# Half-token scans for the first and last image, LayerNorms in lanes of their own, one activation ring, residuals by rows and ranking by image in a scheduled Mamba block

## The chip, the cores and the metric

The kernel runs on one core of one Trainium2 chip. The metric is device time in microseconds (us) of one execution. Times quoted are medians of an experiment's runs with their range. All runs here were in the same state (none of the slow kind), so runs are compared as they are. Sets of runs fell on different chips; the kernel before, run in each set, had medians of 3881 to 3885 us. Engines: PE is TensorE (PEld its weight loads), DVE is VectorE, ACT is ScalarE, POOL is GpSimd.

## The reference, cut to what matters

Eight images of 384 channels and 32x32 pixels (1024 tokens) pass through a Mamba block with an MLP; then five of them pass through an FFN with binarised weights and absmax quantisation.

```python
x = x + conv_block(_ln_c(x))                  # images of 384 x 1024, 8 of them
# inside conv_block (a second LayerNorm comes first):
xz = t @ in_proj_w.T                          # 384 -> 2 x 768
xm, z = jnp.split(xz, 2, axis=-1)
xc = silu(causal_conv3(xm) + conv_b)
dbc = xc @ x_proj_w.T                         # dt (24), B (16), C (16)
dt = softplus(dt @ dt_proj_w.T + dt_proj_b)
dA = exp(dt * A); dBu = dt * xc * B           # 768 channels x 16 states
def step(hst, inp):                           # over 1024 tokens
    hst = dA_t * hst + dBu_t
    return hst, einsum('bdn,bn->bd', hst, C_t)
y = (ys + xc * D) * silu(z)
t = y @ out_proj_w.T
t = gelu(t @ mlp_w1.T + mlp_b1) @ mlp_w2.T + mlp_b2   # 384 -> 1536 -> 384
# the FFN, on images 0 to 4, each a group with its own absmax
h = quantise(_ln_t(t) @ sign(W1 - mean).T + b1)       # 384 -> 1536
t = t + quantise(gelu(h) @ sign(W2 - mean).T + b2)    # 1536 -> 384
def quantise(a):                              # gamma is the max of |a| over one image
    return clip(a * 128 / (gamma + 1e-5), -128 + 1e-5, 128 - 1e-5)
```

## The kernel before

The kernel writes its operations down as a list (`Plan.add`), each with an engine, a cost in us and the tiles that it reads and writes. `Plan.run` then simulates the engines with these costs and emits the instructions of each engine in the order that the simulation finds. The order is then fixed in the program.

```python
MM = 0.86            # us for one product of 128 x 512
SIGNAL = 0.1
LOAD_TABLE = 1.29
...
def choose(e, now, able):                      # in Plan.run
    able = [op for s, op in able if s <= now]
    ...
    if e in ("DVE", "POOL"):
        able = [op for op in able if op.prio[0] > 0] or able
    return min(able, key=lambda op: op.prio)
...
def write_down(self):
    for b in range(B):
        plan.prio = (1,);  self.s1(b)          # LayerNorm, in_proj, convolution, dt, z
        plan.prio = (0,);  self.s2(b)          # the scans
        plan.prio = (2,)
        if b == 0: self.binarise("W1", KC, HID); self.binarise("W2", KH, C)
        self.s3(b)                             # out_proj and MLP
        if b < NQ: self.ffn(b)
```

Tiles come from rings of buffers; MLP, FFN and binarisation share three of them:

```python
"back": ring("back", 3), "t_b": ring("t_b", 3), "w_b": ring("w_b", 3),
"w6": ring("w6", 3), "res": ring("res", 3), "small": ring("small", 24),
```

A scan tile is 32 channels x 4 states on the partitions, 1024 tokens long. ScalarE makes the exponentials into PSUM, GpSimd the products dtx x B, VectorE scans and multiplies by C, and TensorE sums the states, two tiles to a group of sums. There are 96 tiles an image, 768 in all, in 384 groups of sums. Names in the profiles: da are the exponentials and then the scanned states, u the products before and after a scan, py the sums, yg the gated result of the scans; p_in and p_z are the two parts of in_proj, p_out is out_proj, p_h and p_o are the two products of the MLP, p_y and p_y2 those of the FFN; w_b and w6 are weights; p_sum and p_r belong to a LayerNorm.

```python
self.act(... AF.Exp, 1.12, r=[dt_r], w=[da], table="exp", scale=...)      # da is in PSUM
add("POOL", 2.36, lambda: nc.gpsimd.tensor_mul(u.real, dtx_r.real, bq.real))
add("DVE", 2.29, lambda: nc.vector.tensor_tensor_scan(
    da.real, da.real, u.real, 0.0, ALU.mult, ALU.add))
add("DVE", 1.21, lambda: nc.vector.tensor_mul(u.real, da.real, cq.real))
...
self.plan.prio = (-1,)
add("PE", 0.9, sums, r=hcs, w=[py])            # four matmuls, the fold over states
```

The ends of the FFN, shortened: a maximum over all partitions by GpSimd, and the residual of half an image in one instruction. With `lock`, the simulation keeps VectorE and GpSimd apart.

```python
def quant_scale(self, mx, n):
    nc.vector.tensor_reduce(m1.real, mx.real, AX.X, ALU.max)
    nc.gpsimd.partition_all_reduce(m2.real, m1.real, P, bass_isa.ReduceOp.absmax)
    ...
# at the end of ffn, for each half image
self.clip(yh, parts, q2)                       # GpSimd
add("DVE", c_dve(KC * T), lambda: nc.vector.scalar_tensor_tensor(
    x1.real, yh.real, q2.real[:, 0:1], x1.real, ALU.mult, ALU.add
), r=[q2, *parts], w=[x1], lock=True)          # 128 x 1536
```

## Time and profile before

| kernel before | |
|---|---|
| time, median of 4 runs | 3880.9 us (3879.5 to 3887.7) |
| first scan begins | 158.6 us |
| scan stage (first scan to last product behind a scan) | 3542.4 us, VectorE busy 3065.3, idle 477.1 |
| tail (after the last product) | 182.2 us, TensorE busy 161.6, VectorE 5.3 |
| granted TensorE clock, mean | 0.914 |

The page and the views that show this stand in the prediction below. The way of reading is the sum: time = first scan + VectorE's work in the scan stage + VectorE's idling in it + tail. It holds exactly, because the stages follow each other, and it says for every microsecond in which of four terms it was won or lost. Two groups of the kernel before that the prediction does not show matter later; they are by form, with busy us and mean ns after the first bar:

```profile
L885 DVE SCALAR_TENSOR_TENSOR x<-y,q,x 128x1536 f32<-128x1536 f32 x10 | 29.4, 2943 | 35.8 <-POOL y L809 35.6 <-DMA x<-mid_d 0.2
...
L774 DVE TENSOR_TENSOR w<-w,sgn 128x1535 f32<-128x1535 f32 x3 | 5.3, 1757 | 0.1
```

The first is the FFN's residual, ten instructions of 2.9 us; the second a part of the binarisation. Both read two operands from SBUF.

### The profile page before, as it was taken

The numbers are of one execution on the slowest core, as the hardware profiler recorded it, in microseconds if no ns is written. First come the engines' busy times: TensorE is split into PE (matmuls) and PEld (weight loads), VectorE is DVE, ScalarE is ACT, GpSimd is POOL, SyncE is SP. The second block draws the span as 40 slices with busy tenths as digits, with TensorE's granted clock in tenths as the row PEclk, the third lists the DMA queues.
The fourth block names the chain that finished last, engine by engine and source line by source line (L and its number), as shares of the span: only waits on it lengthen the run. The fifth ranks groups of instructions, "written<-read, shape, count | busy, mean of one in ns | idle before, by whom it ended". The sixth has DMA issues, their size and how long they took to land. (4 is left out here: it accounts for less than half of the span.)

```text
span 3883.2 us, 31296 instructions
## 1 busy us (share of the span) xinstructions
PE 3359.5 (87%) x9928; PEld 1275.0 (33%) x9928; DVE 3139.6 (81%) x2291; ACT 1925.0 (50%) x1991; POOL 2114.2 (54%) x1006
## 2 busy tenths in 40 slices
PE   5778878999999798987889978988879877999979
PEld 2223323333333233332233322333323322333334
DVE  5488888888888787897889977898778988899910
ACT  3456565757566665444345443453435443444411
POOL 0346655655555565655656565564666566566600
PEclk7888889999999899998999978998889988999989
DMA  7856667666677676646575564646565456666432
GB/s 252 250 158 205 195 194 250 218 210 198 195 258 245 196 225 196 218 145 204 171 221 174 190 198 154 222 152 206 171 195 179 156 193 192 210 190 189 149 83 81
DMA packets 344740, 746.16 MB, mean 192 GB/s; under 512 B 31488, under 2 KB 100608, under 8 KB 344576
## 3 DMA queue, kind: packets, MB, share of 16 engines
q1 hardware_dynamic: 342704, 743.30, 60.5%
q8 instruction: 79, 1.29, 0.1%
q10 hardware_dynamic: 1872, 0.88, 0.1%
q14 instruction: 85, 0.70, 0.1%
HBM read 560.55 MB, written 183.50 MB: 192 GB/s over the span
## 5 line engine op out<-in xcount | busy, mean ns | idle before, releaser
L628 POOL TENSOR_TENSOR u<-dtx_r,bc 128x1024 f32<-128x1024 f32 x768 | 1803.2, 2367 | 1308.2 <-PE py L643 1161.6
L631 DVE TENSOR_TENSOR_SCAN da<-da,u 128x1024 f32<-128x1024 f32 x768 | 1757.5, 2288 | 261.3 <-ACT da L396 205.8
L396 ACT ACTIVATE da<-dt_r,a_neg 128x1024 f32<-128x1024 f32 x768 | 851.8, 1115 | 977.7 <-DVE u L634 957.3
L634 DVE TENSOR_TENSOR u<-da,bc 128x1024 f32<-128x1024 f32 x768 | 936.6, 1220 | 32.7 <-DVE da L631 1.4
L643 PE MATMUL py<-u,fold 128*32 128x512 f32 x3072 | 547.1, 648 | 242.8 <-DVE u L634 239.2
L380 PE MATMUL p_h<-t,w_b 128*128 128x512 f32 x1152 | 531.8, 613 | 37.1 <-DMA w_b<-in_mlp_w 36.9
L380 PE MATMUL p_o<-g,w 128*128 128x512 f32 x1152 | 511.9, 598 | 0.0
L380 PE MATMUL p_y<-gf,w 128*128 128x512 f32 x720 | 336.9, 623 | 13.3 <-ACT gf L396 13.3
L380 PEld LDWEIGHTS p_h<-t,w_b 128*128 128x128 f32 x1152 | 217.1, 194 | 347.0 <-issue 298.5
L380 PE MATMUL p_y<-tn,w_b 128*128 128x512 f32 x720 | 326.1, 605 | 0.0
L396 ACT ACT_TABLE_LOAD x237 | 304.1, 1283 | 33.5 <-DVE xc L518 17.7
L380 PEld LDWEIGHTS p_o<-g,w 128*128 128x128 f32 x1152 | 213.6, 190 | 295.0 <-issue 284.6
L380 PE MATMUL p_z<-t,w_f 128*128 128x512 f32 x576 | 275.1, 629 | 24.5 <-DMA w_f<-in_in_proj_w 15.2
L380 PE MATMUL p_in<-t,w_f 128*128 128x512 f32 x576 | 271.5, 627 | 26.8 <-ACT t L396 14.8
L380 PE MATMUL p_out<-yg,w 128*128 128x512 f32 x576 | 271.9, 627 | 12.9 <-DMA yg<-yg_d 12.9
L643 PEld LDWEIGHTS py<-u,fold 128*32 128x32 f32 x3072 | 77.8, 111 | 621.8 <-DVE u L634 377.0
L396 ACT ACTIVATE g<-p_h,v_mlp_b 128x512 f32<-128x512 f32 x192 | 128.2, 681 | 192.1 <-PE p_h L380 192.0
L380 PEld LDWEIGHTS p_y<-gf,w 128*128 128x128 f32 x720 | 139.7, 199 | 216.5 <-issue 187.1
L380 PEld LDWEIGHTS p_y<-tn,w_b 128*128 128x128 f32 x720 | 135.0, 193 | 185.7 <-issue 156.1
L396 ACT ACTIVATE y<-p_y,v_b 128x512 f32<-128x512 f32 x150 | 101.9, 683 | 176.9 <-PE p_y L380 136.2
L558 POOL TENSOR_TENSOR xc<-xc,dt 128x512 f32<-128x512 f32 x96 | 118.6, 1269 | 119.0 <-ACT dt L396 119.0
L704 DVE SCALAR_TENSOR_TENSOR res<-p_o,v_mlp_b,res 128x512 f32<-128x512 f32 x48 | 35.2, 733 | 175.5 <-PE p_o L380 175.4
(75 smaller groups left out, 2132.8 us busy)
## 6 DMA issues: line engine op xcount, KB each, us to landing
dt_r<-dt_d SPq DMA_DIRECT2D x192, 512.0 KB, 5.3
dtx_r<-dtx_d SPq DMA_DIRECT2D x192, 512.0 KB, 4.7
w_f<-in_in_proj_w SPq DMA_DIRECT2D x192, 192.0 KB, 3.2
w_b<-in_mlp_w SPq DMA_DIRECT2D x192, 192.0 KB, 3.4
w<-in_mlp_w SPq DMA_DIRECT2D x96, 384.0 KB, 4.0
bc<-rows_d SPq DMA_DIRECT2D x64, 512.0 KB, 6.0
y_d<-y SPq DMA_DIRECT2D x120, 256.0 KB, 3.6
gf<-y_d SPq DMA_DIRECT2D x20, 1536.0 KB, 9.0
```

The lines of the kernel that those rows point to most:

```text
L380: self.nc.tensor.matmul(p.real, w.real[:, k, :], t.real[:, k0 + k, :], start=start and k == 0, stop=stop and k == n - 1,)
L396: lambda: self.nc.scalar.activation(out(), in_(), func, **{k: v() if callable(v) else v for k, v in kw.items()}),
L558: add("POOL", c_pool(T), lambda k=k, xc=xc, dt=dt: nc.gpsimd.tensor_mul(xc.real[:, k, :], xc.real[:, k, :], dt.real[:, k, :]), r=[dt[k]], ...
L628: add("POOL", 2.36, lambda u=u, dtx_r=dtx_r, bq=bq: nc.gpsimd.tensor_mul(u.real, dtx_r.real, bq.real), r=[dtx_r, bq], w=[u])
L631: add("DVE", 2.29, lambda da=da, u=u: nc.vector.tensor_tensor_scan(da.real, da.real, u.real, 0.0, ALU.mult, ALU.add), r=[u], w=[da])
L634: add("DVE", 1.21, lambda da=da, u=u, cq=cq: nc.vector.tensor_mul(u.real, da.real, cq.real), r=[da, cq], w=[u])
L643: nc.tensor.matmul(py.real[p0 : p0 + DQ, :], self.fold, hc.real[:, cols], start=(q == 0), stop=(q == NQUAD - 1),)
L704: nc.vector.scalar_tensor_tensor(res.real, po.real, self.mlp_b2[:, m : m + 1], res.real, ALU.add, ALU.add)
```

## The change

Its intent: start the scans earlier and shorten the tail by scanning the first and the last image in two halves of 512 tokens, with the state carried over in a small tile; and let the order follow the images more evenly. LayerNorms get lanes (their own place in a ring's order), ranking holds the first stage of far-off images back, MLP and FFN share one large activation ring, and the FFN's residual is added by rows of 128 channels. The diff, cut to its core:

```diff
+SUMS = 1.2
...
+        def rank(op):
+            lane, b = op.prio[:2]
+            if lane <= 0:
+                first = (lane, b)
+            elif lane in (1, 4):
+                first = (1, b) if b <= scanned + 1 else (3, b)
+            else:
+                first = (2, b)
+            return (*first, op.prio[2])
...
-            "back": ring("back", 3), "t_b": ring("t_b", 3), "w_b": ring("w_b", 3),
-            "w6": ring("w6", 3), "res": ring("res", 3), "small": ring("small", 24),
+            "yg": ring("yg", 1), "hid": ring("hid", 1), "t_b": ring("t_b", 1), "w_b": ring("w_b", 4),
+            "w6": ring("w6", 2), "res": ring("res", 3),
+            "t_n": ring("t_n", 2), "w6_n": ring("w6_n", 2), "small": ring("small", 12),
...
     def s1(self, b):
+            with self.plan.lane(4):
+                self.load(t, lambda x: x, src, size=4 * P * KC * T)
+                self.norm(t, self.eps_m, (1.0 + E2) / C)
...        (z of the first half is now made between the two dt stages)
     def s2(self, b):
+        if b in (0, B - 1):
+            state = self.piece("state", [P, NJ * NQUAD], "state")
+            for half in range(2):
+                self.scan(b, half, state)
+        else:
+            self.scan(b, None, None)
...        (scan_tile: a tile of a half scan is two blocks of 512 columns)
+        for k, col in enumerate(cols):
+            add("DVE", 0.13 + n * 0.0021, lambda k=k, col=col: nc.vector.tensor_tensor_scan(
+                to.real[:, k, :], da.real[:, k, :], u.real[:, k, :],
+                state.real[:, col : col + 1] if half else 0.0, ALU.mult, ALU.add,
+            ), ...)
+        if half == 0:
+            add("ACT", 0.25, lambda: nc.scalar.copy(state..., to.real[:, :, n - 1]), ...)
...
-                add("PE", 0.9, sums, r=hcs, w=[py])
+                    add("PE", SUMS, sums, r=hcs, w=[py])
...        (binarise)
+            first = self.dram["dtx", 0][0]
+            self.load(w, lambda t: t, src[:, i * kk : (i + 1) * kk, :], r=[first], ...)
...        (ffn)
+            with self.plan.lane(6):
+                ... self.norm(t, self.eps_f, 1.0 / C)
...
-            add("DVE", c_dve(KC * T), lambda yh=yh, x1=x1: nc.vector.scalar_tensor_tensor(
-                x1.real, yh.real, q2.real[:, 0:1], x1.real, ALU.mult, ALU.add
-            ), r=[q2, *parts], w=[x1], lock=True)
+            for m in range(KC):
+                add("DVE", c_dve(T), lambda m=m, yh=yh, x1=x1: nc.vector.scalar_tensor_tensor(
+                    x1.real, yh.real[:, m, :], q2.real[:, 0:1], x1.real, ALU.mult, ALU.add
+                ), r=[q2, yh[m]], w=[x1], lock=True)
...        (write_down: priorities carry the image, FFN and binarisation are lane 5)
```

## The prediction

> **What bounds the kernel now.** I read the page from the top: busy shares, the slices, the chain, the groups. First the shares and the slices (busy tenths of forty 97 us slices):
>
> ```profile
> PE 3359.5 (87%) x9928; PEld 1275.0 (33%) x9928; DVE 3139.6 (81%) x2291; ACT 1925.0 (50%) x1991; POOL 2114.2 (54%) x1006
> ...
> PE   5778878999999798987889978988879877999979
> ...
> DVE  5488888888888787897889977898778988899910
> ...
> PEclk7888889999999899998999978998889988999989
> ```
>
> TensorE and VectorE are both nearly full and neither is full throughout. VectorE is empty in the last two slices and both are half empty in the first. So I asked for busy time by stretch: up to the first scan (158.6 us), from there to the last product behind a scan (3701 us), and the rest. Columns: stretch, length, then busy us (and instructions) of PE, PEld, DVE, ACT, POOL, then granted clock, DMA share, GB/s.
>
> ```profile
> 0.00:158.60 158.60, 99.71 (x238) 42.92 (x238) 68.99 (x123) 55.94 (x69) 17.80 (x20) 0.74 0.78 254
> 158.60:3701.00 3542.40, 3098.26 (x9330) 1161.95 (x9330) 3065.33 (x2161) 1837.03 (x1887) 2095.10 (x986) 0.92 0.61 195
> 3701.00:3883.20 182.20, 161.57 (x364) 70.13 (x364) 5.25 (x7) 32.01 (x35) 1.26 (x1) 0.93 0.32 87
> ```
>
> The reader sees three stages: a head of 159 us before any scan, a scan stage of 3542 us in which VectorE works 3065 us and idles 477 us, and a tail of 182 us that is TensorE alone. What the scan stage is made of stands in the groups (busy, mean ns of one, idle before and what ended it):
>
> ```profile
> L631 DVE TENSOR_TENSOR_SCAN da<-da,u 128x1024 f32<-128x1024 f32 x768 | 1757.5, 2288 | 261.3 <-ACT da L396 205.8
> L634 DVE TENSOR_TENSOR u<-da,bc 128x1024 f32<-128x1024 f32 x768 | 936.6, 1220 | 32.7 <-DVE da L631 1.4
> ```
>
> Scan and product take 1757.5 + 936.6 = 2694 of VectorE's 3140 us. Of its 477 us of idling in this stage the waits view names most:
>
> ```profile
> DVE da L631 <- ACT da L396: 205.8, 78, 13.9
> ...
> DVE m L798 <- POOL m L793: 65.5, 10, 9.6
> ...
> DVE x L885 <- POOL y L809: 35.6, 5, 7.6
> ...
> DVE xr L652 <- PE py L643: 33.1, 21, 5.9
> ```
>
> The tail is read from the chain that ended last, in order of time: the last yg goes out and comes back, then two image halves pass through TensorE, one after the other.
>
> ```profile
> 3707.17 8.56 DMA yg<-yg_d
> 3715.78 17.51 PE p_out L380 x36
> 3733.29 15.46 PE p_h L380 x36
> 3748.77 9.00 DMA w_b<-in_mlp_w
> 3757.91 13.46 PE p_h L380 x24
> 3771.37 30.90 PE p_o L380 x72
> 3802.27 15.45 PE p_out L380 x36
> 3817.72 30.90 PE p_h L380 x72
> 3848.62 30.91 PE p_o L380 x72
> ```
>
> My reading: in the scan stage VectorE is the bound, helped to its idling by TensorE, whose static order also serves MLP and FFN; in the tail TensorE is.
>
> **What the Trainium skill says.** (1) "TensorE: Matmul & The Clock Gate", Part 1 (the HAM clock gate): an idle array falls back to half its clock, activity releases it. The trace agrees: the stretch from 2700 to 2800 us with PE busy 74.7 of 100 us had a granted clock of 0.78, the one from 3400 to 3500 us with 98.4 had 1.00. So evening out TensorE's work saves some of its time. (2) "GPSIMD Engine Reference", section 2.1 Instruction dispatch: a freshly loaded library kernel costs about 6 us without a visible instruction. Here each PARTITION_ALL_REDUCE takes 0.41 us but GpSimd stands idle 5.85 us before the last one and 7.16 us after it; that is where the 65.5 us of "DVE m" come from. (3) "ScalarE: Activation LUTs", What ACT_TABLE_LOAD costs: about 1283 ns each, which is the page's mean (237 of them). The ACT lists before and after hold the same number of loads, 238, so nothing is gained there.
>
> **The change part by part.** The orders of instructions of both kernels are what I used besides the trace.
>
> Tail. With the last image scanned by halves, the order after the last sums holds one half (18 matmuls p_out, 36 p_h, 36 p_o) where there were two. In the trace the second half took 15.45 + 30.90 + 30.91 = 77.3 us. So the tail falls from 182 to about 105 us: 15 us of yg out and back, 17.5 + 15.5 + 13.5 + 30.9 = 77.4 us of matmuls, the rest for waits on weights, GELU and the last store. Gain: some 77 us, the surest part.
>
> Head. Image 0 starts on its first half. Before, dtx of the first half was ready at 76 us, dtx of the second went out at 134.4 us and GpSimd could start at 156.25 us, so store and load cost 22 us. After: 77 + 22 + 2.4 (first product on GpSimd) = some 101 us; but VectorE's order puts ten binarisation sums, whose loads now wait for the first dtx, ahead of the first scan; I take 110 us. That looks like 49 us, but VectorE used the old head to do 69 us of work, the binarisation of the FFN weights included; only about 33 us of it remain ahead of the first scan. The other 36 us move into the scan stage. Net gain some 10 us.
>
> Cost of halves. 192 tiles (two images) scan 512 columns twice. The scan of 1024 takes 2288 ns; taking 0.13 us as fixed part, as the kernel's own constants do, two of 512 cost about 0.15 us more with the gap between them: 192 x 0.15 = 29 us more on VectorE, on the path. ACT gets its exponentials in twos as well, but ACT is at 50%.
>
> Ranking by image, LayerNorms as lanes. Before, the first stage of all images (in_proj, convolution, dt) ran ahead as fast as it could: the p_z work of all eight images is over soon after 1500 us, though the scans of images 3 to 7 (counted from 0) start only at 1595 us. After that TensorE had too little in some stretches and too much in others. I counted from the orders TensorE's work between each 48 scan tiles, at 0.86 us a matmul of 128x512. Before it goes 219, 227, 236, 208 us early and alternates between some 155 and 185 late; after it is near 190 to 220 up to image 5 and then drops to 98 to 180. VectorE's share of such a stretch is 175 to 210 us in both. The sum of the larger of the two over the stretches is nearly the same (about 2970 and 2990 us for all but the first); what can fall is what comes on top, now 340 us. That was 8 to 16 us for a stretch of plain MLP and 30 to 47 us for one that holds an FFN's second half, with its two reductions on GpSimd and its clips. Those ten reductions and the clips remain.
>
> One ring for MLP and FFN activations, w6 from three buffers to two plus two. These pay for the lanes. They make MLP and FFN take turns, so TensorE has fewer things to do in a bubble; with TensorE some 83% needed this costs little on VectorE's path. Residuals by rows: the same bytes and the same VectorE time in smaller pieces; nothing either way.
>
> Sum. Up to the first scan 110; VectorE's work in the scan stage 3140 + 29 - 33 - 3 = 3133; its idling there, now 477, I take as 400 (the named waits for ACT 206 to 160, LayerNorm and py waits down by some 30, reductions and clips unchanged); tail 105. 110 + 3133 + 400 + 105 = 3748, said as 3745 us.
>
> **The rivals.** First: TensorE becomes the bound. Up to image 5 its work equals VectorE's in most stretches, so stalls of one add to those of the other, and turns on the one big activation tile leave bubbles in which the clock falls. For it: from 1000 to 1300 us of the kernel before, with TensorE 88 to 96% busy, VectorE idled 10 to 18%. Against it: the PE work as a whole is unchanged. Idling would stay at 480 or rise to 550; time 3830 to 3900 us. Second: the even load works better than I think, the exponentials come on time and idling falls to 280 us: 3630 us. For it: plain MLP stretches already run with VectorE 92 to 94% busy; against it the unchanged reductions. Third: transfers. With two w6 buffers and the in-order DMA queue, TensorE could wait for weights; the queue's busy share of 60% and only 37 us of waits for w_b before speak against more than 30 us.
>
> **Range and chances.** Tail and head are worth some 87 us less 29 of the halves, so 58 us are fairly certain, 1.5%. The 2% line is 3804 us; it needs some 20 us more out of idling, which I think likely but not sure, as a fixed order that fits a model of costs need not fit the chip. Slower by 2% needs over 200 us of new idling: unlikely. Range 3630 to 3850, chances 0.72, 0.25, 0.03.
>
> **What would show it.** In the profile after: the first scan near 110 us and the last chain with one p_out, p_h, p_o sequence, 100 to 110 us after the last scan product; scans of 512 near 1.2 us each; p_z spread up to the scans of image 5 or 6; "DVE m" still waiting for GpSimd some 65 us in ten times; idling of VectorE between first scan and last product near 400 us. The prediction is wrong if that idling is below 300 or above 480 us, or if waits for weights or for sums rise so that the granted clock falls below 0.9.

## The result, and the profile after

The kernel after takes 3821.7 us (3808.3 to 3825.9, 4 runs) against 3880.9 us: ratio 0.984, with a 95% interval of 0.981 to 0.987. A ratio, here and below, is the mean time of one kernel's fast runs over that of the other's of the same rounds, so it is not quite the ratio of the medians. The result is inside the predicted range, but the gain is 59 us where 136 were forecast, and not over 2%. The page after, same rows as before:

```profile
PE 3355.5 (88%) x9928; PEld 1257.5 (33%) x9928; DVE 3219.0 (84%) x2503; ACT 1983.2 (52%) x2279; POOL 2118.1 (55%) x1006
...
PE   7787898998978999889998999898998998599858
...
DVE  2888899997888998789988799888997899999990
...
PEclk8888998998989999999999999999998999599969
```

VectorE's nearly empty slices at the end shrank from two to one and the scans start in the second slice. But VectorE's busy time rose by 79 us, from 3139.6 to 3219.0, for the same arithmetic. The stages, busy time by stretch (length, then busy us and instructions of PE, PEld, DVE, ACT, POOL, then granted clock, DMA share, GB/s):

```profile
0.00:103.40 103.40, 75.85 (x196) 31.43 (x196) 36.36 (x53) 38.43 (x53) 19.65 (x17) 0.85 0.59 192
103.40:3719.40 3616.00, 3197.97 (x9548) 1190.95 (x9548) 3179.68 (x2447) 1928.22 (x2209) 2097.17 (x988) 0.92 0.62 199
3719.40:3819.20 99.80, 81.64 (x184) 35.15 (x184) 3.00 (x5) 16.59 (x18) 1.26 (x1) 0.89 0.28 78
```

Set against the prediction's sum, term by term:

| us | before | predicted | after |
|---|---|---|---|
| first scan begins | 158.6 | 110 | 103.4 |
| VectorE's work in the scan stage | 3065.3 | 3133 | 3179.7 |
| VectorE's idling in the scan stage | 477.1 | 400 | 436.3 |
| tail | 182.2 | 105 | 99.8 |
| sum | 3883.2 | 3748 | 3819.2 |

Both ends came out as predicted or better. The two middle terms are off by 47 and 36 us, and that is the whole miss. The tail, from the chain that ended last (start, us, what):

```profile
3726.57 8.96 DMA yg<-yg_d
3735.67 17.92 PE p_out L405 x36
3753.59 30.90 PE p_h L405 x72
3784.49 30.91 PE p_o L405 x72
```

One half image is left where the prediction's chain of before shows two. Where VectorE's extra work is, by form (busy us, mean ns, then idle before it and what ended that):

```profile
L751 DVE TENSOR_TENSOR_SCAN da<-da,u 128x1024 f32<-128x1024 f32 x576 | 1317.7, 2288 | 127.7 <-ACT da L421 105.7 <-POOL u L747 17.7 <-POOL xr L718 2.8
L751 DVE TENSOR_TENSOR_SCAN da<-da,state,u 128x512 f32<-128x512 f32 x192 | 246.9, 1286 | 18.8 <-ACT da L421 14.0 <-POOL u L747 1.6
L751 DVE TENSOR_TENSOR_SCAN da<-da,u 128x512 f32<-128x512 f32 x192 | 235.5, 1226 | 39.2 <-ACT da L421 29.5 <-POOL u L747 3.6 <-POOL xr L718 2.4
...
L996 DVE SCALAR_TENSOR_TENSOR x<-y,q,x 128x512 f32<-128x512 f32 x30 | 49.8, 1701 | 39.9 <-POOL y L917 26.1 <-issue 9.2 <-DMA x<-mid_d 4.6
...
L883 DVE TENSOR_TENSOR w<-w,sgn 128x1535 f32<-128x1535 f32 x3 | 8.2, 2745 | 0.1
```

A scan of 1024 cost 2288 ns; two of 512 cost 1226 + 1286 = 2512 ns, the second with its start value read from the state tile. All scans together rose from 1757.5 to 1800.1 us, by 42.6. The residual went from 10 x 2.94 = 29.4 us to 49.8 us, though it moves the same bytes. The binarisation's three element-wise forms took 11.8 us more in sum, at the same sizes, and the small edge corrections of the convolution 6.5 us more. The residuals, the edges and two of the three forms of the binarisation read two operands from SBUF; the third form, a subtraction of a column of scalars from one tensor (w<-w,mean), has 3.2 of the 11.8 us. What they have in common shows in VectorE's timeline of the kernel after (start, us):

```profile
94.14 0.75 DVE L560 TENSOR_TENSOR edge<-halo,conv_w 128x6 f32<-128x6 f32 x1
94.92 2.27 DVE L561 TENSOR_TENSOR xc<-xc,edge 128x6 f32<-128x6 f32 x1
97.23 2.27 DVE L560 TENSOR_TENSOR edge<-halo,conv_w 128x12 f32<-128x12 f32 x1
99.53 0.17 DVE L561 TENSOR_TENSOR xc<-xc,edge 128x12 f32<-128x12 f32 x1
```

and in GpSimd's timeline of the same stretch:

```profile
87.90 11.57 POOL L747 TENSOR_TENSOR u<-dtx_r,bc 128x1024 f32<-128x1024 f32 x5 [21.19 <-DMA w_f<-in_in_proj_w]
```

GpSimd's five products run from 87.9 to 99.5 us. Until then two edge instructions, of six or twelve elements a partition, take 2.27 us each, about as long as one product (2.37 us on average), and the one before them takes 0.75 us and ends at 94.89 us, near the end of the third of five equal products (94.84 us, an estimate from these lines); once GpSimd is done the same kind takes 0.17 us. The residual shows the same within this one trace:

```profile
2142.95 2.30 DVE L996 SCALAR_TENSOR_TENSOR x<-y,q,x 128x512 f32<-128x512 f32 x1 [0.45 <-DMA x<-mid_d]
2155.49 0.75 DVE L996 SCALAR_TENSOR_TENSOR x<-y,q,x 128x512 f32<-128x512 f32 x1 [3.44 <-DMA x<-mid_d]
```

GpSimd multiplies from 2139.1 to 2147.5 us, beside the first of these, and stands idle from 2154.3 to 2166.4 us, beside the second. So the smaller piece is not slow by itself: 0.75 us alone, 2.30 us beside GpSimd. The Trainium skill, "SBUF — State Buffer", section "SBUF: two separate sides", says that an instruction of VectorE with two SBUF inputs and one of GpSimd that reads SBUF exclude each other for a whole instruction. This trace agrees, with 2.27 against 0.17 us and 2.30 against 0.75 us. The wait is booked as busy time, so no row of waits shows it.

VectorE's named waits after:

```profile
DVE da L751 <- ACT da L421: 149.2, 59, 8.7
...
DVE m L907 <- POOL m L902: 51.3, 10, 7.4
...
DVE x L996 <- POOL y L917: 26.1, 4, 7.2
```

The waits for exponentials fell from 205.8 to 149.2 us. The ten waits for GpSimd's maxima and those for its clips are still there.

The early start of the scans can be followed by counting products of 128x1024 behind scans (image 0 is 96 of them). The first 48 were done at 391 us before and at 444 us after, the first 192 (two images) at 1092 and 1152 us. So a lead of 55 us at the first scan had become a lag of 60 us two images later. The kernel after had done more other work by then: by the 192nd product 60 us more of TensorE's.

### The profile page after: what moved, and what is told of

Read it like the earlier page. It is cut to its first block, busy times and chain, and to the rows that moved or that the text cites. A ratio compares the mean times of both kernels' runs of the same rounds, so it can differ in the third digit from the quotient of the medians.

```text
span 3819.2 us, 32052 instructions
## 1 busy us (share of the span) xinstructions
PE 3355.5 (88%) x9928; PEld 1257.5 (33%) x9928; DVE 3219.0 (84%) x2503; ACT 1983.2 (52%) x2279; POOL 2118.1 (55%) x1006
## 5 line engine op out<-in xcount | busy, mean ns | idle before, releaser
L751 DVE TENSOR_TENSOR_SCAN da<-da,u 128x1024 f32<-128x1024 f32 (+1 forms) x768 | 1553.2, 2022 | 166.9 <-ACT da L421 135.2
L421 ACT ACTIVATE da<-dt_r,a_neg 128x1024 f32<-128x1024 f32 (+1 forms) x960 | 903.1, 946 | 983.5 <-DVE u L764 949.9
L686 PE MATMUL py<-u,fold 128*32 128x512 f32 x3072 | 562.8, 659 | 194.4 <-DVE u L764 194.0
L405 PE MATMUL p_y<-gf,w_n 128*128 128x512 f32 x720 | 336.5, 621 | 34.6 <-DMA w_n<-bin_w 15.9
L405 PE MATMUL p_in<-t,w_f 128*128 128x512 f32 x576 | 281.6, 636 | 21.9 <-issue 5.4
L405 PE MATMUL p_out<-yg,w 128*128 128x512 f32 x576 | 269.5, 622 | 33.3 <-DMA yg<-yg_d 21.8
L751 DVE TENSOR_TENSOR_SCAN da<-da,state,u 128x512 f32<-128x512 f32 x192 | 246.9, 1286 | 18.8 <-ACT da L421 14.0
L405 PEld LDWEIGHTS p_y<-gf,w_n 128*128 128x128 f32 x720 | 138.3, 198 | 235.0 <-issue 178.4
L549 DVE SCALAR_TENSOR_TENSOR xc<-p_in,conv_w,xc 128x511 f32<-128x511 f32 x192 | 140.5, 739 | 59.1 <-ACT xc L421 49.4
```

Of the source, the lines that this page charges most:

```text
L405: self.nc.tensor.matmul(p.real, w.real[:, k, :], t.real[:, k0 + k, :], start=start and k == 0, stop=stop and k == n - 1,)
L421: lambda: self.nc.scalar.activation(out(), in_(), func, **{k: v() if callable(v) else v for k, v in kw.items()}),
L549: nc.vector.scalar_tensor_tensor(xc.real[:, m, s:], pm.real[:, : T - s], tap[2 - s], xc.real[:, m, s:], ALU.mult, ALU.add,)
L686: nc.tensor.matmul(py.real[p0 : p0 + DQ, :], self.fold, hc, start=(q == 0), stop=(q == NQUAD - 1),)
L751: add("DVE", 0.13 + n * 0.0021, lambda k=k, col=col: nc.vector.tensor_tensor_scan(to.real[:, k, :], da.real[:, k, :], u.real[:, k, :], sta ...
```

## The experiments

Eighteen kernels ran, each correct against the reference. Unless said otherwise an edit is to the kernel after. Times are medians (range), ratios are to the kernel before of the same rounds.

**What an order's luck is worth.** Any edit changes the static order a little. Two null edits, which change no work and hardly a cost, measure this.

```diff
-SIGNAL = 0.1
+SIGNAL = 0.11
```

> Control of the luck of an order: after, with the scheduler's time for a signal at 0.11 us where it was 0.10, a change of no meaning that makes another order. If an order's luck is small against what was seen (65 us for the cost of the sums, 25 us for the ranking): 3806 to 3836 us. If it isn't, more than 20 us off 3821 us in either direction.

Measured: 3802.0 us (3800.9 to 3805.1), ratio 0.979.

```diff
-LOAD_TABLE = 1.29
+LOAD_TABLE = 1.30
```

> A second control of the same kind: after, with a table load at 1.30 us where it was 1.29. Same expectation: 3806 to 3836 us if luck is small; else more than 20 us off.

Measured: 3834.7 us (3827.7 to 3841.5), ratio 0.988. With the kernel after at 3821.7, three orders of the same program spread over 33 us, though the runs of one order agree within some 20. VectorE's idling in the scan stage was 415.6 and 445.9 us in the two, and 436.3 in the kernel after. I therefore trust a single difference below only from some 40 us up, and a smaller one only where two pairs agree or where a term of the sum shows it directly.

**The halves, one at a time.**

```diff
-        if b in (0, B - 1):
+        if b == B - 1:
```

> After, but only the last image is scanned by halves. Theory A (halving the first image costs more than its early start brings: 21 us of scan time, and the binarisation pushed among the products of GpSimd): the first scan starts near 150 us, VectorE's work falls by 20 to 35 us from 3219, the 48th tile is done before 430 us instead of at 444, the time is 3780 us (3765 to 3800). Theory B (the slow start comes from lanes and ranking, and the halved first image helps by its 40 us earlier start): the time rises to 3840 us or more.

Measured: 3778.1 us (3773.2 to 3781.9), ratio 0.973, as theory A said, though the first scan began at 157.9 us and the 48th tile was done only at 437 us.

```diff
-        if b in (0, B - 1):
+        if b == 0:
```

> After, but only the first image is scanned by halves. Both theories: the tail is again two halves, some 180 us, so about 80 us more, less 21 us of scan work of the last image: 3880 us (3860 to 3900), so no better than the kernel before. If it is much faster than that, the tail is not what the halving of the last image brings.

Measured: 3853.1 us (3851.6 to 3856.4), ratio 0.993. The tail came back, 176.3 us, but the time is below the expected 3860 to 3900: a miss.

```diff
-        if b in (0, B - 1):
+        if b < 0:
```

> After without any halves: lanes, ranking, ring and rows alone. Theory A: VectorE's work 3219 - 43 = some 3175 us, tail 180 us, time 3840 to 3865 us, so the order alone is worth 15 to 40 us over before. Theory B (lanes and ranking lose in the first stretch): 3880 us or more.

Measured: 3819.1 us (3807.2 to 3823.1), ratio 0.983. A miss too: both theories had said 3840 us or more. These four kernels differ in the halves alone, and the sum says where each goes:

| us | first scan | VectorE's work | idling | tail | time |
|---|---|---|---|---|---|
| no halves | 158.3 | 3116.0 | 370.0 | 176.9 | 3819.1 |
| last image only | 157.9 | 3136.8 | 385.1 | 100.3 | 3778.1 |
| first image only | 101.2 | 3149.9 | 423.8 | 176.3 | 3853.1 |
| both (after) | 103.4 | 3179.7 | 436.3 | 99.8 | 3821.7 |

The last image's halves gain 77 us of tail and pay 21 us of VectorE's work and 15 us of idling: 41 us gained, and 31 us when the first image is halved too. The first image's halves start the scans 57 us earlier and pay 34 us of VectorE's work in the scan stage (22 of them displaced from the head) and 54 us of idling: 34 us lost, and 44 us when the last image is halved too. Two pairs agree for each. **The two together bring nothing: 3822 against 3819 us without any halves.** The early start did not last: with the last image alone halved, the first 48 products were done at 437 us although the scans started 55 us later, against 444 us in the kernel after; the first 192 at 1097 against 1152 us. VectorE's idling up to then was 97 us there and 147 us in the kernel after. Of those 50 us, 16 are waits of LayerNorms for their sums on TensorE (5.8 to 21.8 us) and 9 are waits for GpSimd's products (5.6 to 14.1 us). That the first stage of image 1 competes with an early image 0 is my reading of them; no run separates it.

**The last image alone, in the old order.** The kernel before, with the new scan code for the last image only, the old cost of 0.9 and nothing else.

```diff
+        if b == B - 1:
+            state = self.piece("state", [P, NJ * NQUAD], "state")
+            for half in range(2): self.scan(b, half, state)
+        else: self.scan(b, None, None)
```

> The kernel before with the last image scanned by halves as the only change (sums still told as 0.9 us). My term for the tail, by itself: tail 100 us where it was 182, VectorE's work 21 us more, so 3820 us (3800 to 3840). If the order of before leaves other work for the end, the tail stays above 130 us and the time above 3845 us.

Measured: 3841.6 us (3838.7 to 3848.6), ratio 0.990: 40 us gained, as in the new order (41 and 31). Its tail is 129.6 us, between the two expectations, so in the old order some other work is still left for it, and 14 of the 40 us are less idling (462.5 us). Three pairs now say 31 to 41 us for this part.

**The binarisation back in the head.**

```diff
-        if b in (0, B - 1):
+        if b == B - 1:
...
-            first = self.dram["dtx", 0][0]
-            self.load(w, lambda t: t, src[...], r=[first], ...)
+            self.load(w, lambda t: t, src[...], ...)
```

> As the run with only the last image by halves, and in addition the loads of the FFN weights for binarisation no longer wait for the first dtx, as in the kernel before. Theory A: the binarisation runs in the head while GpSimd is idle, so its subtractions take 1.75 us again and not 2.3 to 2.7, and VectorE has work in the head: 10 to 25 us below the run with only the last image by halves, 3765 us. Theory B: no difference beyond 5 us.

Measured: 3775.0 us (3770.5 to 3784.2), ratio 0.972. Theory A missed: it had said 10 to 25 us below the 3778 us of the last image only, and it was 3, which is nothing (theory B). The durations did come back:

```profile
L882 DVE TENSOR_TENSOR w<-w,sgn 128x1535 f32<-128x1535 f32 x3 | 5.3, 1757 | 0.1
```

That is the 1757 ns of the kernel before instead of 2745, at the same size. VectorE's work in the scan stage fell by 28 us, of which the first scan (164.5 us) took 7 back and idling 18. So the displaced binarisation explains busy time, not measurably the end time.

**Residuals with one operand in PSUM.** ScalarE scales a row block into PSUM, and VectorE adds it to the other operand.

```diff
-                add("DVE", c_dve(T), ... nc.vector.scalar_tensor_tensor(
-                    x1.real, yh.real[:, m, :], q2.real[:, 0:1], x1.real, ALU.mult, ALU.add
-                ), r=[q2, yh[m]], w=[x1], lock=True)
+                py2 = self.piece("mm", [P, T], "p_res")
+                self.act(py2.real, yh.real[:, m, :], AF.Identity, c_act(T), scale=q2.real[:, 0:1])
+                add("DVE", c_dve(T), ... nc.vector.tensor_add(
+                    x1.real, py2.real, x1.real), r=[py2], w=[x1])
```

> After, but the last residual of the FFN is scaled by ScalarE into PSUM and VectorE adds PSUM and x1, so VectorE's instruction has one operand in SBUF where it had two. Theory A (an instruction of VectorE with two SBUF operands is held up while GpSimd works): the 30 additions take some 0.74 us each where they took 1.70, VectorE's work falls by some 28 us to 3190 us, the time by 10 to 35 us from 3821 us. Rival (they are long for another reason, such as smaller pieces): they stay above 1.2 us each and the time within 10 us.

```profile
L1001 DVE TENSOR_TENSOR x<-p_res,x 128x512 f32<-128x512 f32 x30 | 20.0, 685 | 52.5 <-ACT p_res L421 32.6 <-DMA x<-mid_d 11.5 <-issue 8.3
```

Measured: 3787.4 us (3780.9 to 3793.4), ratio 0.974, 34 us below the kernel after. Each addition takes 685 ns instead of 1701, so 1.0 us of each residual was waiting, and the 30 of them account for 30 us of VectorE's busy time. The edit also changes the operation and takes the plan's `lock` away, but the 0.75 us of an unchanged residual beside an idle GpSimd, shown above, says that neither is needed for a short one. Its work in the scan stage fell by 32.8 us; idling rose by 6. The gain in time lies within what two orders can differ by, but the term it should show in shows it. The other obvious repair, the residual on GpSimd itself, was not run.

**Ranking and lanes.**

```diff
         def rank(op):
+            lane = {4: 1, 5: 2, 6: 2}.get(op.prio[0], op.prio[0])
+            return (lane, op.prio[2])
```

> After, but operations are ranked as before (first stage of any image ahead of MLP and FFN of any image). If ranking by image is what the order gains (62 us in the run without halves): p_z is over early again, idling of VectorE in the scan stage rises from 436 us to 460 or more, time 3850 to 3880 us. If the gain comes from lanes and rings: within 10 us of 3821 us.

Measured: 3796.0 us (3786.5 to 3803.8), ratio 0.977. A miss: 3850 to 3880 us or no change was expected, and it was 26 us faster than the kernel after.

```diff
-            with self.plan.lane(4):
+            with self.plan.lane(1):
...
-            with self.plan.lane(6):
+            with self.plan.lane(5):
```

> After, but each LayerNorm is in the lane of its stage again. If the lanes of their own gain: waits of VectorE around p_sum and p_r rise by 15 us or more and the time to 3840 to 3860 us. If they don't: within 10 us of 3821 us.

Measured: 3818.8 us (3816.1 to 3822.7), ratio 0.983: the lanes alone are worth nothing measurable. My theory had been that ranking by image gives the even load and with it the smaller idling. It fell here: idling without ranking was 421.8 us, not more than the 436.3 with it. The lead to the 62 us by which even the kernel without halves beats the kernel before came from a run, the sums at 1.5 us. It was meant as a control of an order's luck and was 65 us off; the null edits, the 0.9 and the 1.8 were then run to tell a cause from luck.

**The cost of a group of sums.** In the kernel after, sums take 562.8 us of TensorE in 384 groups, 1.47 us a group (before: 547.1 us, 1.42). The kernel before plans them at 0.9, the kernel after at 1.2.

```diff
-SUMS = 1.2
+SUMS = 0.9
```

> After, with the group of sums told as 0.9 us, as the kernel before has it; the trace of after shows 1.47 us. If the order's gain with 1.5 us (65 us) is from telling the right cost, the gain goes the other way here: 3850 us or more, with idling of VectorE in the scan stage above 450 us. If it was luck: anywhere, and as likely below 3821 us.

Measured: 3900.1 us (3888.3 to 3904.6), ratio 1.004.

```diff
-SUMS = 1.2
+SUMS = 1.5
```

> Control: after, with the scheduler told that a group of sums takes 1.5 us, about what the traces show, where it is told 1.2. Nothing else changes but the order that falls out. If the chance of one order is small: 3806 to 3836 us. If it is off by more than 20 us, differences of that size between other variants are no evidence by themselves.

Measured: 3756.2 us (3746.8 to 3762.0), ratio 0.967.

```diff
-SUMS = 1.2
+SUMS = 1.8
```

> After, with the group of sums told as 1.8 us, more than the 1.42 to 1.47 us that the traces show. If what helps is a plan near the truth: no better than with 1.5 us, 3750 to 3800 us. If what helps is to keep TensorE's other work thin among the sums at any cost: lower still, idling of VectorE below 370 us, 3730 us or less.

Measured: 3787.3 us (3779.0 to 3796.6), ratio 0.975. The scan stages at 0.9 and at 1.5, and the four kernels in the terms of the sum:

```profile
102.50:3801.50 3699.00, 3212.43 (x9548) 1192.17 (x9548) 3196.76 (x2447) 1947.36 (x2225) 2095.74 (x988) 0.90 0.61 194
102.50:3660.50 3558.00, 3158.48 (x9512) 1184.51 (x9512) 3181.05 (x2445) 1954.88 (x2230) 2099.61 (x988) 0.93 0.63 201
```

| planned cost | VectorE's work | idling | tail | time |
|---|---|---|---|---|
| 0.9 | 3196.8 | 502.2 | 99.4 | 3900.1 |
| 1.2 (after) | 3179.7 | 436.3 | 99.8 | 3821.7 |
| 1.5 | 3181.1 | 377.0 | 99.6 | 3756.2 |
| 1.8 | 3178.4 | 332.0 | 165.7 | 3787.3 |

The instructions are the same in all four; only the number in the plan differs. Idling falls by 45 to 66 us with every step of 0.3, each step more than the 30 us between the null edits, and **with the old 0.9 the whole rest of the change gains nothing** (0.4% slower than the kernel before, 16 us, which is within an order's luck). At 1.8 the tail grows by 66 us: MLP work was left over. The way I read it is that a plan which thinks the sums cheap puts more MLP and FFN products between them than fit, so sums, and behind them scans, come late; a plan which thinks them dear leaves these products for the end. The idling and the tails are measured; this reading of them is argued. One row speaks for it: GpSimd's waits for sums in the scan stage fall from 1307 us at 0.9 to 1261, 1139 and 991 us. Of the four costs tried, the best is 1.5, near the 1.47 us that the trace of the kernel after measures for a group.

Does the number do it without the rest? In the kernel before:

```diff
-                add("PE", 0.9, sums, r=hcs, w=[py])
+                add("PE", 1.5, sums, r=hcs, w=[py])
```

> The kernel before with one number changed: the group of sums told as 1.5 us where it was 0.9. If the right cost is what helps an order: 3800 to 3850 us, 30 to 80 us below before, so more than the whole change's order brought. If it was luck with the changed kernel alone: within 20 us of 3881 us or worse.

```profile
3595.60:3920.20 324.60, 308.57 (x710) 135.01 (x708) 9.76 (x13) 62.26 (x68) 1.26 (x1) 0.98 0.36 99
```

Measured: 3920.4 us (3914.3 to 3922.8), ratio 1.009. A miss: 3800 to 3850 us was expected. Idling fell by 94 us, to 383.1 (in the kernel after, from 0.9 to 1.5, by 125). But the tail, this stretch, went from 182 to 325 us, with TensorE busy for 309 of them. The number moves waiting out of the scans in both kernels; only in the new order is the work it displaces done before the scans end. Which of the new parts sees to that? One run asked the ranking:

```diff
 SUMS = 1.5, and as in the run without ranking:
+            return (lane, op.prio[2])
```

> After with sums told as 1.5 us and the old ranking. With the kernel before the right cost left a tail of 325 us (e12). If ranking by image is what keeps the tail at 100 us: tail above 130 us and 3790 us or more. If lanes, rings and half scans do: tail 100 us and 3735 to 3775 us, as with the ranking by image (3756 us).

Measured: 3718.3 us (3713.0 to 3725.6), ratio 0.958, below both expectations, with a tail of 99.9 us: not the ranking. Against 3756.2 with ranking it is 38 us faster, the second pair of the same sign (26 us above). So ranking by image is not what gains, and it may well cost 25 to 40 us; with two null edits 33 us apart I leave it at "may". What keeps the tail short at 1.5 is then the halves of the last image, the rings or the lanes in them; that stays open.

**The maxima on GpSimd.** Next to the exponentials, the largest waits of VectorE by name in the scan stage are those for the ten maxima, which the change did not touch. What they do to GpSimd, in the kernel before:

```profile
3267.66 0.41 POOL L793 PARTITION_ALL_REDUCE m<-m  x1 [5.85 <-issue]
3275.23 2.33 POOL L628 TENSOR_TENSOR u<-dtx_r,bc 128x1024 f32<-128x1024 f32 x1 [7.16 <-issue]
```

Some 13 us of idling (in brackets) around an instruction of 0.41 us. The ten of them have 73.6 us of it before and 80 us after them. The maximum by TensorE instead: a product with the identity turns the column into a row, VectorE takes its maximum, a product with ones spreads it.

```diff
-        nc.gpsimd.partition_all_reduce(m2.real, m1.real, P, bass_isa.ReduceOp.absmax)
+        nc.tensor.matmul(row.real[0:1, :], m1.real, self.ident, start=True, stop=True)
+        nc.vector.tensor_reduce(top.real[0:1, :], row.real[0:1, :], AX.X, ALU.max)
+        nc.tensor.matmul(col.real, self.ones[0:1, :], top.real[0:1, :], start=True, stop=True)
```

> After, and only the ten maxima across partitions moved from GpSimd's library operation to TensorE and VectorE. In e14 this took 108 us. If that is GpSimd's own cost (some 10 us idle at each of 10, and what waits behind it): 80 to 120 us below 3821 us here too, 3700 to 3740 us. If in e14 it was helped by the other changes: less than 60 us.

Measured: 3686.0 us (3683.1 to 3693.1), ratio 0.950: 136 us below the kernel after, more than the 80 to 120 expected, with idling at 307.7 instead of 436.3 us. The waits row "DVE m" names 51 us of it. The rest are waits that the stalls of GpSimd, or the order planned with its maxima, cause elsewhere; which of the two I did not separate.

**The parts that pay, together.** Last image only in halves, binarisation in the head, sums at 1.5, residual through PSUM:

```diff
 the edits of "binarisation back in the head" (which has the last image only),
 "residuals with one operand in PSUM" and SUMS = 1.5
```

> All that the runs so far point to: after with only the last image by halves, binarisation free of the first dtx, sums told as 1.5 us, and the FFN residual through PSUM. If the parts add (46 us for the first two, 65 us for the cost of the sums, 34 us for the residual, all below 3821 us): 3676 us, within 25 us for the luck of the order. If they eat the same idling: 3720 us or more.

Measured: 3690.3 us (3684.3 to 3692.7), ratio 0.950; idling 344.4 us.

```diff
 the same, and the maxima by TensorE
```

> As the run before in this call, and the ten maxima across partitions are taken by two small matmuls and a reduction on VectorE where GpSimd ran a library operation with some 6 us of idling before and after. The waits for it and the knock-on waits (50 us for the maxima, part of the 26 us for clips) fall: 40 us below that run, 20 to 80. If GpSimd's idling is hidden behind other work: within 20 us.

```profile
164.20:3479.80 3315.60, 3086.99 (x9439) 1163.68 (x9437) 3073.52 (x2285) 1895.74 (x2068) 2084.87 (x976) 0.95 0.66 209
```

Measured: **3582.7 us (3578.0 to 3585.9), ratio 0.922** (0.920 to 0.924), better than both kernels. This is the scan stage: VectorE busy for 3074 of 3316 us, so it idles 242 us, about half of the 477 before; the maxima alone made 102 of the 344 go away, and 108 us of time where 20 to 80 were expected. The tail is 99.8 us and the mean granted clock 0.946.

## Why the prediction was right or wrong, point by point

**Tail: right.** Predicted 182 to 105, measured 182.2 to 99.8 us, with the predicted single sequence of products. The run with the last image alone in the old order shows 40 us net for it.

**First scan: right. Net gain of the head, "some 10 us": wrong.** The scans began at 103.4 us, predicted 110. The step that failed is "Net gain some 10 us", which took only the displaced work off the lead. The runs with one image halved each show 34 to 44 us of loss in its place: the early stage costs 54 us of extra idling, which the working did not have at all.

**"Cost of halves" 29 us: mis-sized.** It is 42.6 us. The fixed part was taken from the kernel's constants; the trace has 1226 and 1286 ns for the two scans of 512, so 0.22 us a tile and not 0.15.

**"Residuals by rows: ... nothing either way": wrong.** It cost 20 us of VectorE's time. Counting bytes was the failure: the step did not ask which instructions have two operands in SBUF and so wait for GpSimd. Ten chances to wait became thirty; the run with one operand in PSUM takes the wait away (1701 to 685 ns).

**"The other 36 us move into the scan stage": right in kind, too small.** The moved binarisation and the edges became dearer by 18 us beside a busy GpSimd. With the two points above, 13.6 + 20.4 + 18.3 = 52 us against the forecast for VectorE; 47 is the measured miss of that term, the rest being small differences elsewhere.

**"Its idling there, now 477, I take as 400": wrong by 36 us, and for a wrong reason.** What the step left out is what the halves themselves do: without them idling was 370.0 us, below the forecast, and with both it is 66 us more. In the rows of waits the same shows as falls that came and rises that were not thought of. In the scan stage the waits for exponentials fell by 57 us (46 predicted), those of LayerNorms and for py by 12 (30 predicted), those for maxima and clips by 24 (none predicted); all others rose by some 45 us, GpSimd's products from 6 to 23 and the loads and issues of the smaller residuals from 0 to 14 among them. p_z did spread out, until some 3000 us, as predicted, and idling fell. But the reason given, ranking by image and LayerNorm lanes, is not supported: without the one and without the other idling was 421.8 and 424.8 us, not above 436.3, and the null edits alone moved it between 415.6 and 445.9. The cost of the sums, which the prediction never mentions although the diff has it, is worth 66 us of idling between 0.9 and 1.2; with the old 0.9 idling is 502 us, above the 477 of the kernel before. "Reductions and clips unchanged" held roughly as a row (65.5 to 51.3 us for the reductions), but the row understates them: taking the reductions away gave 108 to 136 us.

**The rivals.** TensorE as the bound was the nearest of them: its 3830 us is 8 us from the result, but idling fell instead of staying at 480, so its mechanism is not what happened. The even load at 280 us of idling did not come with this change; other edits came near it (307.7 and 242 us). Weights: the granted clock stayed at 0.92 in the scan stage, so nothing like the feared drop below 0.9 occurred, and the matmuls' waits for w_b were 3.1 us, where they had been 36.9. A rival was missing from the list: that a planned cost in the scheduler decides the order.

**Not settled.** What the rings, the two plus two w6 buffers and the clips' planned cost, which the diff lowers too (3.51 to 2.89 us for 3072 elements), are worth was not isolated; nor was the kernel without halves run at 0.9, so that the 62 us of the order are the number's doing is inferred from the runs with halves. The idling of an early first image is located (in the first two images) but only half of it is named.

## What to carry to other kernels

Split the time into head, the bound engine's work, its idling, and tail, and follow every forecast gain through all four: here a start 55 us earlier was paid back within two images. In a statically scheduled kernel compare each planned cost with its duration in the trace before reasoning about priorities, and run null edits so that you know what the luck of an order is worth. Look for two-operand SBUF instructions of VectorE beside a busy GpSimd, and for library calls on a GpSimd that feeds the main loop: here both cost more than any row of waits shows.

## What the Trainium skill lacked or had wrong

- "SBUF — State Buffer", section "SBUF: two separate sides": agreed, but it gives no size for the loss of many small instructions. Here a 0.17 us edge instruction took 2.27 us, and 30 residuals, 0.75 us beside an idle GpSimd and 0.69 us with one operand in PSUM, took 1.70 us each. It also does not say that the profile books the wait as VectorE's busy time.
- "GPSIMD Engine Reference", section "2.1 Instruction dispatch": names about 6 us for a freshly loaded kernel, and the trace has 5.85 to 9.55 us before the ten reductions of 0.41 us. It does not give the way back, 7.03 to 11.54 us of idling before the next instruction, so the stall is about double. In this kernel ten such reductions were worth 108 to 136 us.
- No page I read gives the fixed cost of a scan or of its start value from a tile: 1226 ns for 512 columns from zero, 1286 ns from a tile, 2288 ns for 1024.
